# Attention scores of a two-layer graph network: each product of 128 keys made as two of 64 keys

## The chip, the core and the metric

The kernel runs on one core of a Trainium2 chip. Its time is the device time of one execution in microseconds (us), the median of several runs. The core has TensorE (in the profile PE for matrix products and PEld for the loading of their weights), VectorE (DVE), ScalarE (ACT), GpSimd (POOL) and SyncE (SP, which issues DMAs here). Matrix products read SBUF and write PSUM[...].

## What is computed

x has 16 graphs of 1,024 nodes with 256 features; adj is a 1,024 by 1,024 matrix. There are two layers, each added to its input. The change lies in the attention of the first; all of it is in f32.

```python
# --- layer 0 ---
h = jnp.maximum(_layernorm(x, axis=-1), 0.0)
...
Wg = adj[None, :, :] * A_s
g = jnp.einsum('bcn,bnm->bcm', fea, Wg)
g = jax.nn.relu(g * para.reshape(1, C, N))
q = jnp.transpose(g, (0, 2, 1)).reshape(B, N, h, hd).transpose(0, 2, 1, 3)
kv = (x @ kv_w).reshape(B, N, 2, h, hd).transpose(2, 0, 3, 1, 4)
k, v = (kv[0], kv[1])
scale = (1.0 + 1e-06) / (np.sqrt(hd) + 1e-06)
attn = jax.nn.softmax(jnp.einsum('bhnd,bhmd->bhnm', q, k) * scale, axis=-1)
out = jnp.einsum('bhnm,bhmd->bhnd', attn, v)
...
# --- layer 1 ---
h = jnp.maximum(_layernorm(x, axis=-1), 0.0)
...
out = h @ W2.T + b2
out = _batchnorm(out, g2, be2)
```

Layer 1 aggregates over the normalised adj and makes two products, each followed by a batch norm. There are 4 heads (h) of 64 features (hd). So for every graph and head the scores are a product over 64 features, of 1,024 queries with 1,024 keys.

## The kernel before

One pass of `layers` does everything. Its long middle part is `attention`, which for graph b makes scores and values, and lays beside them, piece by piece, the work of other graphs: the queries, keys and values of graph b+1 (`queries`, `keys_values`; tiles pg, pk, pv), and the second layer's aggregation and first product of graph b-1 (`aggregate`, `hidden`; tiles pa, py). A last part, `second`, makes the second product of layer 1 after batch norm (tiles m_f), with the reference's batch statistics.

The order of PE's work is written out by hand. `attention` goes through steps. There are 16 graphs, 2 pairs of heads k and 2 blocks f of 512 queries, 64 units in all; a unit has four steps g, each with two blocks m of 128 keys. In a step PE is given, in this order:

- `scores`: for each of the two blocks m a PSUM tile sc of 128 keys by 2 heads by 512 queries (two banks, one for each head e). The keys of a pair of heads lie in the same SBUF tile, head e in partitions 64e to 64e+63, and the queries likewise. So each head's product contracts over 64 rows and uses one half of the array's rows (L890). ACT then takes the exponential of the whole sc tile into pr (L898). The pool of sc has two buffers, so a tile waits for the exponential of the tile before the last.
- at some steps the small products `sums` (L961) and the transposes `ot` (L986) that end the unit before,
- `values` of the step before: the product of pr with the values into o, 128 keys in the rows and 64 features in the columns, one half of the array's columns for each head (L931),
- one or more pieces of the background, by a planner's costs, until the step's due share is done.

DVE adds the exponentials up for the softmax's denominators (L917, L920).

The background's products go through a helper, `product` (L171), which makes every product of 128 output partitions as two of 64, one in each column half of the array. The helper's two calls differ in the output's partitions and the weights' columns:

```python
        def product(dst, left, right, start, stop):
            for e in range(2):
                r = slice(e * HW, (e + 1) * HW)
                nc.tensor.matmul(dst[r], left[:, r], right, start=start, stop=stop)
```

HW is 64, P is 128, FB is 512 and HD is 64. The products of `second` (L1235) are not split. The program's other branch, `layers(True)` with `shifted_attention`, is taken only where the exponentials leave their range, and isn't in the profile.

Of the kernel before, what the change touches and what calls it, by code (L numbers as in the profile page):

```python
# [17 lines left out]
P = 128  # L18
# [5 lines left out]
def gnn_two_layers_kernel(  # L24
# [12 lines left out]
    nc = tc.nc  # L37
# [6 lines left out]
    FB = 512  # L44
# [3 lines left out]
    HW = P // 2  # L48
# [47 lines left out]
    def layers(shifted):  # L96
# [23 lines left out]
        xs, hs, hts, ats, qs, ks, vs = {}, {}, {}, {}, {}, {}, {}  # L120
# [761 lines left out]
        def scores(b, k, f, g):  # L882


            made = []
            for m in (2 * g, 2 * g + 1):
                sc = ps_sc.tile([P, 2, FB], F32, tag="sc", name=f"sc_{b}_{k}_{f}_{m}")
                for e in range(2):
                    r = slice(e * HD, (e + 1) * HD)
                    nc.tensor.matmul(  # L890
                        sc[:, e, :],
                        ks[b][k][r, m * P : (m + 1) * P],
                        qs[b][k][r, f * FB : (f + 1) * FB],
                        start=True,
                        stop=True,
                    )
                pr = p4.tile([P, 2, FB], F32, tag="p", name=f"p_{b}_{k}_{f}_{m}")
                nc.scalar.activation(pr, sc, AF.Exp)  # L898
                made.append(pr)
            return made  # L900
# [107 lines left out]
        def attention():  # L1008
# [7 lines left out]
            for s in range(len(steps) + 2):  # L1016
                if s < len(steps):
                    unit, g = steps[s]
                    b = unit.at[0]
                    if s % per_graph == 0:  # L1020
                        run(bg)
                        top = False
                        bg, done = background(b), 0.0
                        total = (37.6 if b > 0 else 41.0) * (b + 1 < B) + 24.0 * (b > 0) + 6.0 * (b + 2 < B)
                        total += 13.7 * (0 < b < B - 2) + 27.4 * (b == B - 1) + 3.0 * (b == 0)

                        total -= 10.3 * (b == B - 1)
                    made = scores(*unit.at, g)
                    due = total * (s % per_graph + 1) / per_graph
                else:  # L1030
                    due += 5.1
# [408 lines left out]
```

## Time and profile before

| | |
|---|---|
| time, median of 3 runs | 2608.92 us (2606.27 to 2610.16) |
| span of the profiled execution, first to last instruction | 2604.3 us |
| mean granted TensorE clock | 0.991 |
| sc passes (executed matmuls of L890) | 2048 |
| exponentials p (L898, ACT) | 512, mean 1020 ns |
| passes of the values o (L931) | 2048 |
| DMA rate over the span | 140 GB/s |

An f32 product of the program is executed as two passes, each with a weight load of its own: 1,024 score products are 2,048 matmuls and 2,048 weight loads in the profile. The form 64*128 is the rows and columns of the array that a pass uses; 64x512 after it is the moving operand, partitions by elements. Of a group, "busy" is the union of its instructions' times, and "mean" that of one. Matmuls are pipelined and their ends are modelled, so for the pace of PE the starts are to be read.

### The profile page before, as it was taken

How to read it: one execution, taken by the hardware profiler on the slowest of the kernel's cores; microseconds unless marked ns; L12 is line 12 of the kernel's file. 1: busy time of each engine (PE TensorE's matmuls, PEld its weight loads, DVE VectorE, ACT ScalarE, POOL GpSimd, SP SyncE). 2: the span in 40 equal slices, each digit the busy share in tenths (PEclk: the TensorE clock that was granted, in tenths of full speed). 3: DMA queues.
4: the chain of work that ended last, by engine and by line, in shares of the span. 5: the costliest groups of instructions: out<-in, count | busy, mean ns of one | idle time of the engine just before them, and what ended most of it. 6: DMA issues, size and time to landing. Idle time of an engine off the chain costs nothing.

```text
span 2604.3 us, 31375 instructions
## 1 busy us (share of the span) xinstructions
PE 2525.9 (97%) x11627; PEld 931.8 (36%) x11627; DVE 1822.7 (70%) x2837; ACT 1460.7 (56%) x2034; POOL 391.3 (15%) x456
## 2 busy tenths in 40 slices
PE   7999999999999999999999999999999999999994
PEld 3333333333333333333333333333333333334443
DVE  4768686867767686868677676858686776657774
ACT  6774565647474746656464747465564634335543
POOL 1540001000101000010001010000100001036653
PEclk9999999999999999999999999999999999999997
DMA  3654224152524343241525243433315242355459
GB/s 138 229 171 173 93 99 154 54 189 73 182 83 152 111 148 101 102 150 55 183 71 182 86 156 107 147 100 114 137 62 180 66 166 105 109 196 221 170 198 367
DMA packets 130915, 363.46 MB, mean 140 GB/s; under 512 B 15288, under 2 KB 32192, under 8 KB 124608
## 3 DMA queue, kind: packets, MB, share of 16 engines
q1 hardware_dynamic: 110144, 282.70, 31.3%
q0 software_dynamic: 20608, 78.66, 7.9%
q8 instruction: 94, 1.54, 0.2%
q14 instruction: 69, 0.57, 0.1%
HBM read 286.79 MB, written 74.51 MB: 139 GB/s over the span
## 4 chain that ended last, share of the span: by engine, by line
PE 87%; ACT 7%; DMA 2%; issue 2%; DVE 1%; SPq 0%; POOL 0%; POOLq 0%; DVEq 0%; ACTq 0%
PE sc L890 17%; PE o L931 16%; PE pa L171 15%; PE pg L171 14%; PE py L171 8%; PE m_f L1235 7%; PE pk L171 4%; PE pv L171 4%; ACT w L458 3%; DMA out_dram<-xo_f 2%; ACT p L898 2%; PE ot L986 1%; ACT w L466 1%; PE sums L961 1%; ACT ht L399 1%
## 5 line engine op out<-in xcount | busy, mean ns | idle before, releaser
L898 ACT ACTIVATE p<-sc 128x1024 f32<-128x1024 f32 x512 | 495.0, 1020 | 452.5 <-PE sc L890 452.1
L920 DVE TENSOR_TENSOR acc<-acc,p 128x1024 f32<-128x1024 f32 x384 | 472.2, 1230 | 143.2 <-ACT p L898 121.8
L890 PE MATMUL sc<-q,k 64*128 64x512 f32 x2048 | 509.0, 615 | 4.7 <-ACT p L898 4.6
L931 PE MATMUL o<-p,v 128*64 128x512 f32 x2048 | 495.9, 605 | 0.0
L171 PE MATMUL pg<-w,h_a 128*64 128x512 f32 x1600 | 357.9, 592 | 3.1 <-DVE q L612 2.3
L171 PE MATMUL pa<-aht,h_b 128*64 128x512 f32 x1536 | 344.0, 592 | 3.5 <-ACT h_b L341 3.4
L890 PEld LDWEIGHTS sc<-q,k 64*128 64x128 f32 x2048 | 175.9, 186 | 325.5 <-issue 284.4
L458 ACT ACTIVATE w<-cbc,csum 128x512 f32<-128x512 f32 x256 | 285.5, 1168 | 0.0
L171 PE MATMUL py<-at,w 128*64 128x512 f32 x1024 | 232.8, 597 | 8.4 <-ACT ht L399 7.0
L445 DVE SCALAR_TENSOR_TENSOR w<-w,adj 128x1024 f32<-128x1024 f32 x128 | 157.5, 1230 | 114.8 <-ACT w L466 110.8
L931 PEld LDWEIGHTS o<-p,v 128*64 128x64 f32 x2048 | 124.1, 136 | 250.3 <-issue 247.2
L171 PEld LDWEIGHTS pg<-w,h_a 128*64 128x64 f32 x1600 | 114.7, 137 | 232.0 <-issue 214.4
L746 POOL DMA_DIRECT2D y_d<-y x128 | 70.5, 551 | 795.0 <-ACT y L745 787.2
L171 PEld LDWEIGHTS pa<-aht,h_b 128*64 128x64 f32 x1536 | 110.8, 137 | 216.9 <-issue 208.3
L745 ACT ACTIVATE y<-py,vec 128x512 f32<-128x512 f32 x128 | 87.6, 684 | 142.3 <-PE py L171 119.7
L749 DVE BATCH_NORM_STATS2 stats<-y 128x6 f32<-128x512 f32 x128 | 85.7, 687 | 79.6 <-ACT y L745 79.5
L466 ACT ACTIVATE w<-w 128x1024 f32<-128x1024 f32 x128 | 135.2, 1056 | 1.7
L520 DVE TENSOR_TENSOR w<-w,w 128x1024 f32<-128x1024 f32 x112 | 132.8, 1217 | 1.5
L341 ACT ACTIVATE h_b<-x,lnsm_b 128x256 f32<-128x256 f32 x128 | 70.4, 609 | 110.7 <-DVE lnsm_b L330 110.7
L93 POOL TENSOR_SCALAR lnsm_b<-mv_b 128x4 f32<-128x4 f32 x32 | 12.1, 379 | 791.5 <-DVE mv_b L319 791.4
L171 PEld LDWEIGHTS py<-at,w 128*64 128x64 f32 x1024 | 72.2, 137 | 162.4 <-issue 129.8
L171 PE MATMUL pk<-ht,kvw_f 128*64 128x512 f32 x512 | 117.0, 599 | 1.5 <-ACT ht L399 1.5
(158 smaller groups left out, 2779.7 us busy)
## 6 DMA issues: line engine op xcount, KB each, us to landing
aht<-aht_d SPq DMA_DIRECT2D x224, 512.0 KB, 6.3
adj<-in_adj_dram SPq DMA_DIRECT2D x128, 512.0 KB, 4.4
y_d<-y POOLq DMA_DIRECT2D x128, 256.0 KB, 2.6
yin_f<-y_d SPq DMA_DIRECT2D x32, 1024.0 KB, 6.3
x<-in_x_dram SPq DMA_DIRECT2D x32, 512.0 KB, 5.1
para<-in_para_dram SPq DMA_DIRECT2D x64, 256.0 KB, 3.9
x_d<-x POOLq DMA_DIRECT2D x16, 1024.0 KB, 10.3
xo_f<-x_d SPq DMA_DIRECT2D x32, 512.0 KB, 8.6
```

What stands on the lines that cost most here:

```text
L171: nc.tensor.matmul(dst[r], left[:, r], right, start=start, stop=stop)
L445: nc.vector.scalar_tensor_tensor(w, w, 1.0, a, op0=ALU.add, op1=ALU.mult)
L458: nc.scalar.activation(w[:, t, :].rearrange("p (t q) -> p t q", q=P), cbc[:, q * NT // NH : (q + 1) * NT // NH], AF.Abs, bias=csum[:, th * ...
L466: nc.scalar.activation(made[i], made[i], AF.Tanh, scale=-0.5 / C)
L520: nc.vector.tensor_sub(block(i)[part], block(x)[part], block(y)[part])
L745: nc.scalar.activation(y, made, AF.Identity, bias=b1[:, j : j + 1])
L749: nc.vector.bn_stats(stats1[:, j, i, :], y)
L890: nc.tensor.matmul(sc[:, e, :], ks[b][k][r, m * P : (m + 1) * P], qs[b][k][r, f * FB : (f + 1) * FB], start=True, stop=True,)
L898: nc.scalar.activation(pr, sc, AF.Exp)
L920: nc.vector.tensor_add(self.acc, self.acc, pr)
L931: nc.tensor.matmul(self.o[r, :], vs[b][k][:, m, r], pr[:, e, :], start=(m == 0), stop=(m == NT - 1),)
L1235: nc.tensor.matmul(made, left[:, j, :], right[:, j, :], start=(j == 0), stop=(j == JH - 1))
```

## The change

Each score product is made as two. The inner loop takes the keys of a block in two halves of 64 (c), which are the weights of one pass each, and writes them to partitions 0 to 63 and 64 to 127 of the same bank. With the row halves that the two heads use already, a product takes one quarter of the array, 64 rows by 64 columns. The exponential, the values and all else read and write the same tiles as before, and the order of the other instructions is the same on every engine.

```diff
                 sc = ps_sc.tile([P, 2, FB], F32, tag="sc", name=f"sc_{b}_{k}_{f}_{m}")
                 for e in range(2):
                     r = slice(e * HD, (e + 1) * HD)
-                    nc.tensor.matmul(
-                        sc[:, e, :],
-                        ks[b][k][r, m * P : (m + 1) * P],
-                        qs[b][k][r, f * FB : (f + 1) * FB],
-                        start=True,
-                        stop=True,
-                    )
+                    for c in range(2):
+                        part = slice(c * HW, (c + 1) * HW)
+                        nc.tensor.matmul(
+                            sc[part, e, :],
+                            ks[b][k][r, m * P + c * HW : m * P + (c + 1) * HW],
+                            qs[b][k][r, f * FB : (f + 1) * FB],
+                            start=True,
+                            stop=True,
+                        )
                 pr = p4.tile([P, 2, FB], F32, tag="p", name=f"p_{b}_{k}_{f}_{m}")
                 nc.scalar.activation(pr, sc, AF.Exp)
```

## The prediction

> **What bounds the kernel now.** I read the busy shares first, then the groups, then the order of TensorE's work in one stretch of the attention, since a busy PE says nothing yet of where its time goes.
>
> ```profile
> PE 2525.9 (97%) x11627; PEld 931.8 (36%) x11627; DVE 1822.7 (70%) x2837; ACT 1460.7 (56%) x2034; POOL 391.3 (15%) x456
> ```
>
> PE is at 97% and no other engine is above 70%. The windows of the attention (columns: stretch, its length, then busy us and instructions of PE, PEld, DVE, ACT and POOL, then clock and DMA) say the same without the ends:
>
> ```profile
> 600.00:1000.00 400.00, 398.62 (x1910) 141.63 (x1908) 290.97 (x457) 226.09 (x320) 29.23 (x44) 1.00 0.35 123
> ```
>
> So between some 60 and 2,260 us PE sets the pace, at the full clock. PE is also 87% of the chain that ended last, with ACT 7% and issue 2%. The groups by form show how the products are made (x is executed instructions; an f32 product of the program is executed as two passes, each with its own weight load):
>
> ```profile
> L890 PE MATMUL sc<-q,k 64*128 64x512 f32 x2048 | 509.0, 615 | 4.7 <-ACT p L898 4.6
> L931 PE MATMUL o<-p,v 128*64 128x512 f32 x2048 | 495.9, 605 | 0.0
> L171 PE MATMUL pg<-w,h_a 128*64 128x512 f32 x1600 | 357.9, 592 | 3.1 <-DVE q L612 2.3 <-ACT k L632 0.9
> L171 PE MATMUL pv<-kvw_f,ht 128*64 128x256 f32 x1024 | 116.1, 379 | 0.0
> L1235 PE MATMUL m_f<-yin_f,combined_f 128*128 128x512 f32 x128 | 57.5, 592 | 0.0
> ```
>
> The reader is to see two things. A whole product of 128 rows by 128 columns costs two passes at 57.5/128 = 449 ns (m_f, unsplit) or four at 357.9/1600 = 224 ns (pg, column halves): 898 and 895 ns. Splitting by columns alone buys no array time, because two halves run side by side and each pass lasts as long as before. Second, the scores cost 509.0/2048 = 249 ns a pass where pg costs 224. What the 25 ns are is in the order of PE's work (start, length, group, xcount):
>
> ```profile
> 1003.02 5.32 PE L171 MATMUL py<-at,w 128*64 128x512 f32 x24
> 1008.27 1.99 PE L890 MATMUL sc<-q,k 64*128 64x512 f32 x8
> 1010.18 1.94 PE L931 MATMUL o<-p,v 128*64 128x512 f32 x8
> 1011.95 0.60 PE L171 MATMUL py<-at,w 128*64 128x512 f32 x2
> ```
>
> Read the starts, not the lengths (the ends carry a modelled tail). In the steady state a pair of passes starts every 429 ns: 12 pairs of py should take 5.15 us and take 5.25 until sc starts, so about 0.09 is lost on the way from column halves to row halves. Four pairs of sc should take 1.72 and take 1.91; four of o take 1.77 and pass into py, also in column halves, with nothing lost. What the sc run loses lies at its two ends. The durations of single passes split it up:
>
> ```profile
> L890 PEld LDWEIGHTS sc<-q,k x2048: 182/186/187, 61.6 to 2261.2; 64*128 64x128 f32 x187
> L890 PE MATMUL sc<-q,k x2048: 589/589/693, 61.6 to 2261.6; 64*128 64x512 f32 x187
> L931 PEld LDWEIGHTS o<-p,v x2048: 132/137/137, 67.1 to 2267.5; 128*64 128x64 f32 x187
> L931 PE MATMUL o<-p,v x2048: 592/592/644, 67.1 to 2268.0; 128*64 128x512 f32 x187
> ```
>
> (minimum/median/maximum in ns.) The longest score pass is 693 - 589 = 104 ns over the usual one, the longest o pass 644 - 592 = 52: at the start of a run nothing hides the weight load, and 128 columns cost 104 where 64 cost 52. Taken over the whole trace every run of scores is 8 passes long, so there are 2048/8 = 256 runs, and their 693s are 2 passes a run. From its first pass to the next instruction a run lasts 1.918 us: 4 x 0.429 = 1.716, the load 0.104, and some 0.09 until the array is empty for the next shape. That is 256 x 1.918 = 491 us, 19% of the span, on PE's path.
>
> **What the Trainium skill says.** TensorEngine Tiling (Array Packing), Key Properties: changing the tiling mode, not just the tile, drains TensorE, and tiles work independently. The trace agrees on the drain: about 0.09 us each way. TensorE: Matmul & The Clock Gate, LDWEIGHTS: a load takes its columns divided by 1.2 ns, whatever the rows; for 128 and 64 columns 107 and 53, and the trace has 104 and 52. The same page, Part 3: row and column tiles compose, and sixteen small tiles were measured side by side, while matmuls start strictly in the order of the program. No 64x64 tile stands in this trace, and only two tiles ever run at once, so it can show neither. PSUM Pressure on the tiling page: row tiles must not share a PSUM bank at one time; here e picks the bank and c only the partitions of it, so that is kept.
>
> **The change part by part.** Removed: 1,024 program matmuls of 64 rows by 128 columns. Added: 2,048 of 64 by 64. Order and waits elsewhere stay: the wait for a free sc stands on the first of four instead of the first of two, the signal on the last. Nothing moves on ACT, DVE, POOL or the DMA queues.
>
> 1. Array time. Per score tile there are eight passes instead of four, each still 512 columns of q, 429 ns. If four run side by side that is 2 x 429, as before: 0. The moving operand is then read by four tiles of 64 rows, as many rows as the two tiles of 128 rows in pg, which keep 429.
> 2. Exposed weight load at the start of a run: 104 becomes 52. 256 x 0.052 = -13.3 us.
> 3. Later starts: two neighbouring tiles start 6 to 7 ns apart, so the fourth starts some 20 ns after the first instead of 7. Inside a run each tile keeps its own pace and this vanishes; at the end of a run the next shape waits for the last: 256 x 0.013 = +3.3 us.
> 4. Issue: 16 executed instructions (loads and passes) in 858 ns, 54 ns each. pv already runs 2,048 in 116.1 us, 57 ns each with its tails. Taken at 0; if issue fell short by 5 ns each, 16 x 512 x 0.005 = 41 us would be lost, which is why the range is open upward.
> 5. Drains at both ends of a run: the shapes still differ (64x64 against 128x64 or 128x128). Taken at 0. Bound below: were a change of row halves alone free, 252 entries out of column-split products would save 0.09 + 0.05 and 114 exits into o the same, some -50 us; bound above 0.
> 6. ACT gets sc 13 ns later and 52 ns earlier; DVE follows. Hidden.
>
> Sum -13.3 + 3.3 = -10.0 us. About 9% of the chain is ACT and issue, where a faster PE waits instead (py for ht, sc for p): -9.1. On the profiled execution 2604.3 becomes 2595.2. That execution's span lies 4.6 below the median of 2608.92, which I take for what lies around it: forecast 2599.8.
>
> **Rivals.**
> - *A: the four weight loads don't run side by side.* For: every load in the trace has at most one partner. Against: two row halves load together, and two column halves too. If the row halves of one column half take turns, step 2 is 0 and step 3 stays: +3.3, 2612. If all four take turns, 208 instead of 104: 256 x 0.117 = +30, 2639.
> - *B (slower): the second row half starts a pass late.* Place: the start of each run. The program lists both column halves of row half 0, each two passes, and only then row half 1. If PE interleaves the two passes of neighbours in pairs only and then keeps order, row half 1 starts with the second passes of row half 0. In a run this fills up again, and only its ends stay half empty: one more 429 ns a run. 256 x (0.429 - 0.039) = +100 us, 2709. It decides from a delay of 39 ns. For it: matmuls keep order, and the trace has never interleaved more than two. Against: both tiles of a pair start together on the first pass already, which shows that PE reaches past a second pass that is blocked.
> - *C: the change doesn't do what it says, two passes at a time is all there is.* Every score tile then takes 4 x 429 instead of 2 x 429: 512 x 0.858 = +439, less 13, 3035. For: nothing in the trace has four. Against: two row tiles and two column tiles each work with no loss, and neither the reading (pg) nor the writing (two banks at a time, as now) is more than is shown.
> - *D: the drain gets cheaper too.* Step 5's bound: about 2550. Against: any change of shape costs the same 0.09 in this trace.
>
> **How the numbers follow.** Forecast 46%, A 18%, B 18%, C 14%, D 4%. The likeliest gives 2599.8. Its own range is 2594 (all of step 2, no cost) to 2606 (half of it). The overall range must leave out no more than 2 in 10; with C and D outside it is 2591 to 2714. A measurement of this kernel can tell 0.2%, 5.2 us. Faster by more: 41 of the forecast's 46 and D, 45%. Within: 5 of the forecast and 12 of A, 17%. Slower: 6 of A, B and C, 38%.
>
> **What would show it.** Right: sc passes of 64*64, 16 a run; four starting within some 20 ns; the longest some 52 over the usual; about 1.88 us from the first pass of a run to what follows. A: the longest 104 or more over the usual. B: 2.3 us a run. C: 3.6 us a run and some 900 us of sc. D: py of 24 passes leaving after 5.15 instead of 5.25 us. It would be wrong altogether if passes in steady state were no longer 429 ns apart (issue, or reads that collide).

## The result, and the profile after

| | before | changed |
|---|---|---|
| time, median of 7 runs | 2609.3 us (2606.27 to 2610.16) | 2601.52 us (2599.16 to 2602.98) |
| ratio | | 0.9971, 95% interval 0.996 to 0.9981 |
| span of the profiled execution | 2604.3 us | 2597.8 us |

The changed kernel is faster by 7.8 us, 0.3%. The page after, first the busy shares, then two of its groups (busy us, mean ns of one, idle time before):

```profile
PE 2519.7 (97%) x13675; PEld 887.5 (34%) x13675; DVE 1823.0 (70%) x2837; ACT 1460.5 (56%) x2034; POOL 392.9 (15%) x456
...
L892 PE MATMUL sc<-q,k 64*64 64x512 f32 x4096 | 500.3, 604 | 3.3 <-ACT p L900 3.3
...
L892 PEld LDWEIGHTS sc<-q,k 64*64 64x64 f32 x4096 | 131.4, 132 | 345.4 <-issue 306.4
```

There are twice as many score passes, each about as long as before (mean 604 ns, before 615), and they take slightly less of PE together. So four passes run side by side where two did. The order of PE's work in one stretch (start, length, group, xcount):

```profile
1000.50 5.32 PE L171 MATMUL py<-at,w 128*64 128x512 f32 x24
1005.75 1.95 PE L892 MATMUL sc<-q,k 64*64 64x512 f32 x16
1007.63 1.94 PE L933 MATMUL o<-p,v 128*64 128x512 f32 x8
1009.39 1.89 PE L171 MATMUL py<-at,w 128*64 128x512 f32 x8
```

By the starts, py's 24 passes again take 5.25 us and o's eight 1.76. Only the run of scores is shorter: 1.88 us where it was 1.91. Over all 256 runs the median from the first pass to what follows is 1.878 us, before 1.918. Where the 40 ns lie is seen in the weight loads (PEld). Before (start, length, group, xcount):

```profile
1008.27 0.30 PEld L890 LDWEIGHTS sc<-q,k 64*128 64x128 f32 x4 [0.81 <-issue]
1008.80 0.19 PEld L890 LDWEIGHTS sc<-q,k 64*128 64x128 f32 x2 [0.23 <-issue]
```

and after:

```profile
1005.75 0.21 PEld L892 LDWEIGHTS sc<-q,k 64*64 64x64 f32 x8 [0.81 <-issue]
1006.23 0.15 PEld L892 LDWEIGHTS sc<-q,k 64*64 64x64 f32 x4 [0.28 <-issue]
```

The first row of each holds the loads for the first two passes of every tile; the next load goes in as the second pass begins. That is 0.53 us after the start of the run before and 0.48 after, where 0.43 would be a pass with no load to wait for. By the single instructions, the median starts of a run's passes were 0, 7, 533, 540, 962 ns and so on, and are now 0, 7, 13, 20, then 480, 487, 493, 500, then 909: 53 ns gained, 13 given back by the fourth tile.

Not all of 256 x 0.040 = 10.2 us arrives in the profiled span, which is 6.4 shorter. (The medians differ by more, 7.8. The changed kernel's profiled execution took 2599.8 us, 2.0 more than its span; with the same 2.0, that of the kernel before took 2606.3, near the fastest of its seven.) Cutting PE's time from each start to the next and adding it up by name gives sc 491.1 to 482.5 us, pv 112.3 to 114.3, and all others within 0.4 of before. Two things took something back. First, pv (the values of the next graph) waits for ACT. Of the view of the tile pv, the idle time of PEld that ACT's copy v ended (us, times), before:

```profile
  ACT v L649: 2.8, 13
```

and after:

```profile
  ACT v L649: 5.0, 13
```

pv takes turns in the two PSUM buffers of the background, and its third tile in a graph needs the first copied out by ACT. ACT's work before that copy, in the changed kernel (start, length, group):

```profile
1514.76 1.23 ACT L508 ACTIVATE q<-q 128x512 f32<-128x512 f32 x2 [0.36 <-DVE q L506]
1515.90 1.92 ACT L900 ACTIVATE p<-sc 128x1024 f32<-128x1024 f32 x2
1517.71 0.65 ACT L649 COPY v<-pv 128x256 f32<-128x256 f32 x2
```

The copy comes after two exponentials, and these after two activations of q that waited for DVE. DVE has by then worked for 34.4 us with no pause over 0.3 us, in each of the 13 graphs and in both kernels. By the traces, then, the wait begins at DVE, though its share of the span is 70%, and a faster PE doesn't shorten that stretch. PE has four runs of scores beside it, which save 4 x 0.04 = 0.16 us, and the wait has grown by 2.2/13 = 0.17: what PE saves there is lost whole.

Second, one run of scores fell into a half clock. The windows (stretch, length, busy us of the five engines, granted clock, DMA) of the kernel before:

```profile
167.00:170.50 3.50, 3.17 (x18) 1.68 (x18) 2.81 (x3) 3.50 (x6) 0.00 (x0) 1.00 0.38 137
```

and of the changed one, with the run that it hit below:

```profile
167.00:170.50 3.50, 3.35 (x16) 0.79 (x16) 2.99 (x3) 3.50 (x6) 0.00 (x0) 0.51 0.31 116
```

```profile
167.15 3.59 PE L892 MATMUL sc<-q,k 64*64 64x512 f32 x16 [2.46 <-ACT p L900]
```

From its start to the next instruction at 170.67 us it takes 3.52 us instead of 1.88, a loss of 1.6. So sc should be 10.2 - 1.6 = 8.6 lower, as found.

### The profile page after: what moved, and what is told of

Its sections match the earlier page's. It is cut to its first block, busy times and chain, and to the rows that moved or that the text cites. A ratio compares the mean times of both kernels' runs of the same rounds, so it can differ in the third digit from the quotient of the medians.

```text
span 2597.8 us, 35471 instructions
## 1 busy us (share of the span) xinstructions
PE 2519.7 (97%) x13675; PEld 887.5 (34%) x13675; DVE 1823.0 (70%) x2837; ACT 1460.5 (56%) x2034; POOL 392.9 (15%) x456
## 4 chain that ended last, share of the span: by engine, by line
PE 84%; ACT 7%; DVE 3%; DMA 3%; issue 2%; SPq 0%; POOL 0%; POOLq 0%; ACTq 0%; DVEq 0%
PE sc L892 15%; PE o L933 15%; PE pa L171 15%; PE pg L171 14%; PE m_f L1237 7%; PE py L171 6%; PE pv L171 4%; PE pk L171 4%; ACT w L458 3%; DMA out_dram<-xo_f 2%; ACT p L900 2%; PE ot L988 1%; ACT w L466 1%; DVE acc L922 1%; PE sums L963 1%
## 5 line engine op out<-in xcount | busy, mean ns | idle before, releaser
L892 PE MATMUL sc<-q,k 64*64 64x512 f32 x4096 | 500.3, 604 | 3.3 <-ACT p L900 3.3
L892 PEld LDWEIGHTS sc<-q,k 64*64 64x64 f32 x4096 | 131.4, 132 | 345.4 <-issue 306.4
```

The costliest lines, as they stand in the source:

```text
L892: nc.tensor.matmul(sc[part, e, :], ks[b][k][r, m * P + c * HW : m * P + (c + 1) * HW], qs[b][k][r, f * FB : (f + 1) * FB], start=True, sto ...
```

## The experiments

My theory: the gain is the halved weight load that the start of each run exposes, less the later start of the fourth tile, and the price of every change of the array's shape is left as it was. The rivals are that the order or number of tiles made the gain, that halves are faster in themselves, and that the shape change got cheaper. All diffs are against the changed kernel; each is timed against the kernel before on its own chip, and where two changed kernels are compared, that reference differs by at most 0.5 us.

### Another order of the four quarters

```diff
-                for e in range(2):
-                    r = slice(e * HD, (e + 1) * HD)
-                    for c in range(2):
-                        part = slice(c * HW, (c + 1) * HW)
+                for c in range(2):
+                    part = slice(c * HW, (c + 1) * HW)
+                    for e in range(2):
+                        r = slice(e * HD, (e + 1) * HD)
```

> The four quarters of a score tile in another order: column half 0 of both heads, then column half 1 of both, instead of head by head. My theory (four tiles keep their own pace, only the exposed weight load of a run has changed): first starts again at 0, 7, 13 and 20 ns, a run of scores 1.88 us, the time that of the changed kernel, 2601 us within 3. Rival (it is the neighbours in the program that are interleaved, so the order decides who runs side by side): the second pair starts about one pass later, 2.3 us a run, 2700 us.

Measured: 2601.18 us, ratio 0.9969 (0.9957 to 0.9981). The order of PE's work:

```profile
1007.32 1.95 PE L892 MATMUL sc<-q,k 64*64 64x512 f32 x16
1009.20 1.94 PE L933 MATMUL o<-p,v 128*64 128x512 f32 x8
```

A run is 1.88 us, and its first passes start at 0, 7, 13, 20 and 480 ns, as before the swap. Whichever tiles are neighbours in the program, all four run at once.

### Keys in four quarters

```diff
-                    for c in range(2):
-                        part = slice(c * HW, (c + 1) * HW)
+                    for c in range(4):
+                        part = slice(c * SQ, (c + 1) * SQ)
                         nc.tensor.matmul(
                             sc[part, e, :],
-                            ks[b][k][r, m * P + c * HW : m * P + (c + 1) * HW],
+                            ks[b][k][r, m * P + c * SQ : m * P + (c + 1) * SQ],
```

SQ is 32.

> Keys in four quarters of 32 columns instead of two halves of 64: eight tiles of 64 rows by 32 columns. My theory: the exposed load of a run falls from 52 to about 26 ns, but the eighth tile starts some 47 ns after the first instead of 20, so a run again takes 1.88 us and the time stays at 2601 within 4. Rival 1 (issue is close to its limit): 32 executed loads and passes now fall on 858 ns, 27 ns each; if 54 ns, the most that the trace had shown, is the limit, a run doubles and the time is 3040 us. Rival 2 (the gain came from using more and smaller tiles, not from the load): a further gain of about 8 us, 2593.

Measured: 2602.24 us, ratio 0.9974 (0.9963 to 0.9985). The tile sc (minimum/median/maximum in ns) and a run:

```profile
L892 PEld LDWEIGHTS sc<-q,k x8192: 102/106/107, 63.0 to 2256.8; 64*32 64x32 f32 x200
L892 PE MATMUL sc<-q,k x8192: 589/589/1057, 63.0 to 2257.3; 64*32 64x512 f32 x200
```

```profile
1007.34 1.95 PE L892 MATMUL sc<-q,k 64*32 64x512 f32 x32
1009.21 1.94 PE L933 MATMUL o<-p,v 128*64 128x512 f32 x8
```

The load fell by another 27 ns (133 to 106), and the eighth tile starts 47 ns after the first instead of the fourth 20 ns after it. The two cancel and the run is 1.878 us again. So the gain isn't one of number or smallness of tiles, it is a trade of columns to load against starts in a row, and two halves are as good as four quarters. It also settles issue: 32 loads and passes in 858 ns, 27 ns each, lose nothing.

### Two shapes in one score tile

```diff
-                    for c in range(2):
-                        part = slice(c * HW, (c + 1) * HW)
+                    for c in range(2 - e):
+                        n = HW if e == 0 else P
+                        part = slice(c * n, (c + 1) * n)
```

> Only head 0 is split into two column halves, head 1 stays one product of 64 rows by 128 columns, so that two shapes alternate within a score tile. If any change of shape empties the array and loads anew: head 0 and head 1 no longer run side by side, a run is 8 passes of 0.429 with four drains of 0.09 and four loads (0.052 or 0.104), 4.1 us instead of 1.88, 3170 us. Rival (tiles in separate row halves are free of each other whatever their width): 2605 us.

Measured: 3152.77 us in one run. The order of PE's work:

```profile
1500.85 4.19 PE L893 MATMUL sc<-q,k 64*64 64x512 f32 x12
1504.96 1.51 PE L934 MATMUL o<-p,v 128*64 128x512 f32 x6
```

A run is 4.11 us. The median starts of its passes are 0, 7, 480, 487 (head 0), 1006, 1539 (head 1 alone), 2058 and so on: from 487 to 1006 are a pass of 429 and a drain of 90, and the next 533 are a pass and the 104 of a load of 128 columns. Tiles in separate row halves don't run side by side when their shapes differ. The four quarters are fast because all four have one shape.

### Whole products in the background

```diff
-            for e in range(2):
-                r = slice(e * HW, (e + 1) * HW)
-                nc.tensor.matmul(dst[r], left[:, r], right, start=start, stop=stop)
+            nc.tensor.matmul(dst, left, right, start=start, stop=stop)
```

> The scores as in the changed kernel, but the helper of the background makes whole products of 128 by 128 instead of column halves. My theory (what shape changes and exposed loads cost is all there is): each step now has a change of shape between o and the background, which had none: 252 x (0.09 drain + 0.104 load) = +49 us, 2650. Rival (halves are no better than whole products, a change of columns alone is no change of mode): 2602 to 2606.

Measured: 2644.97 us, ratio 1.0141 (1.0125 to 1.0156), 43 us over the changed kernel where 49 were forecast. The order of PE's work and the passes of pg (minimum/median/maximum in ns):

```profile
1007.40 1.94 PE L931 MATMUL o<-p,v 128*64 128x512 f32 x8
1009.26 5.42 PE L169 MATMUL pa<-aht,h_b 128*128 128x512 f32 x12
1014.61 1.95 PE L890 MATMUL sc<-q,k 64*64 64x512 f32 x16
```

```profile
L169 PE MATMUL pg<-w,h_a x800: 592/592/697, 31.7 to 2127.5; 128*128 128x512 f32 x160
```

o's eight passes now take 1.86 us to the next start instead of 1.76: the drain of 0.09 that a change of shape adds. The first pass of a stretch is up to 105 ns long over the usual: the load of 128 columns, which no pass of another shape hides. In the sum by names o grows by 22 us and the background by 22. A stretch of 12 whole passes takes 5.35 us, of which 0.1 is that load, where 24 halves took 5.25. A change of columns alone is a change of shape too, and no other saving by the halves is seen.

### The sums in the shape of o

```diff
-                nc.tensor.matmul(
+                product(
                     pt,
                     same.rearrange("p a r -> p (a r)"),
                     self.part.rearrange("p e c -> p (e c)"),
-                    start=True,
-                    stop=True,
+                    True,
+                    True,
                 )
```

> The changed kernel, with the product of the sums (128 columns of weights, between a run of scores and the values o) also made in two column halves, the shape of o. My theory (a change of shape costs a drain of 0.09 us and what is exposed of the load): from sums to o there is no change of shape any more and the load falls from 0.10 to 0.05, so the way from the first sums pass to o shrinks from 0.338 us to some 0.17, 49 times; where transposes follow the sums (14 times) there is a new change of shape, 0.1 more. About -9 us, 2592. Rival (such small products in between hide the drain that would be paid anyway, so the way to o stays as long): 2601 us.

Measured: 2594.27 us (2592.05 to 2594.88), ratio 0.9943 (0.993 to 0.9957): the fastest version, 7 us under the changed kernel. The changed kernel's PE around the sums:

```profile
1557.71 1.04 PE L892 MATMUL sc<-q,k 64*64 64x512 f32 x8
1558.68 0.41 PE L963 MATMUL sums<-part,same 128*128 128x32 f32 x2
1559.02 1.94 PE L933 MATMUL o<-p,v 128*64 128x512 f32 x8
```

and this one's:

```profile
1553.30 1.95 PE L892 MATMUL sc<-q,k 64*64 64x512 f32 x16
1555.17 0.31 PE L171 MATMUL sums<-part,same 128*64 128x32 f32 x4
1555.31 1.92 PE L933 MATMUL o<-p,v 128*64 128x512 f32 x8
```

From the sums to o it is 0.14 us instead of 0.34; over the trace the medians are 138 and 338, more than forecast (0.17); that o's own load goes in behind the sums would explain it, but isn't shown by itself. In the sum by names the sums fall from 20.9 to 10.9 us. But pv rises by 3.2, and its wait for ACT's copies grows again:

```profile
  ACT v L649: 10.5, 26
```

This counts both engines, 8.2 us of PEld and 2.3 of PE, in the same 13 places. Each of DVE's stretches is 34.4 us long here too. The shares of the chain that ended last, in the changed kernel and then in this one, show what this means:

```profile
PE 84%; ACT 7%; DVE 3%; DMA 3%; issue 2%; SPq 0%; POOL 0%; POOLq 0%; ACTq 0%; DVEq 0%
```

```profile
PE 60%; DVE 19%; ACT 14%; issue 4%; DMA 3%; SPq 0%; POOL 0%; DVEq 0%; POOLq 0%; ACTq 0%
```

Now PE itself waits, and so the chain runs through DVE: ahead of the pv pass at 1515.13 us it follows DVE from 1478 to 1511, then ACT's activation of q, its exponentials and its copy.

### The second part in column halves

```diff
                 for j in range(JH):
-                    nc.tensor.matmul(
-                        made, left[:, j, :], right[:, j, :], start=(j == 0), stop=(j == JH - 1)
-                    )
+                    for e in range(2):
+                        r = slice(e * HW, (e + 1) * HW)
+                        nc.tensor.matmul(
+                            made[r],
+                            left[:, j, r],
+                            right[:, j, :],
+                            start=(j == 0),
+                            stop=(j == JH - 1),
+                        )
```

> The changed kernel, with the products of the second part (m) also in column halves. They stand in one long sequence of their own shape, so by my theory there is no change of shape and hardly an exposed load to save: the m passes keep 429 ns a pair of halves, the time stays at 2601 within 3 us. Rival (halves are faster in themselves): m takes 202 us of PE's timeline, and a gain of the size that the scores had, 2%, would be 4 us or more, 2597.

Measured: 2601.5 us, ratio 0.9973 (0.9962 to 0.9983), the time of the changed kernel. One group of the changed kernel and the same here (busy us, mean ns):

```profile
L1237 PE MATMUL m_f<-yin_f,combined_f 128*128 128x512 f32 x128 | 57.5, 592 | 0.0
```

```profile
L1239 PE MATMUL m_f<-yin_f,combined_f 128*64 128x512 f32 x256 | 58.0, 592 | 0.0
```

Where no change of shape and no exposed load is to be had, halves bring nothing; m takes 202.5 us of PE's timeline in one and 202.6 in the other.

### DVE copies the first values

```diff
+                copy = nc.vector.tensor_copy if g == 0 else nc.scalar.copy
                 for k in range(CC):
-                    nc.scalar.copy(
-                        vs[b][k][:, 2 * g : 2 * g + 2, :], pv[:, :, k * P : (k + 1) * P]
-                    )
+                    copy(vs[b][k][:, 2 * g : 2 * g + 2, :], pv[:, :, k * P : (k + 1) * P])
```

together with the sums in halves.

> As e5_sums, and the first pair of value tiles of each graph copied out of PSUM by DVE instead of ACT. In the changed kernel the third pv product waits 13 times for ACT's copy of v, 5.0 us where before it was 2.8, since ACT has two exponentials to do first. If that wait is where the part of the gain went that is missing in the sum: the wait falls to 3 us or less and the time by some 2 us against e5_sums. Rival (DVE is later than ACT there, being 70% busy): no gain or a loss of a few us.

Measured: 2649.12 us, ratio 1.0156 (1.0142 to 1.017), 55 us slower than with ACT's copies. The rival was right that DVE is later, and its size was underrated. PE's waits (engine line, releaser: us in total, times, longest):

```profile
PE pv L171 <- DVE v L650: 39.0, 13, 3.0
```

The copies went to the engine whose stretch the wait comes from. In the graph near 1550 us PE could go on at 1554.1, but DVE adds up exponentials until 1556.2 and only then copies; PE waits 3.0 us, and so in all 13 graphs. At the end of 11 of these waits the clock is also halved for 3.4 us. So the wait can't be had back in this way; whether less work for DVE in its stretch, or another order of it, would do so wasn't tried.

## Why the prediction was right

- **What bounds the kernel** held in the main: PE set the pace in the attention, and a saving of 40 ns at 256 places arrived, less 2.0 us at pv and 1.6 at half clock. But once in each of 13 graphs DVE's stretch of 34.4 us sets it.
- **Step 1, array time 0.** Four tiles run side by side, each pass 429 ns. The statement of the Trainium skill, TensorE: Matmul & The Clock Gate, Part 3, that row and column tiles compose, which no run had shown here, holds for f32 passes of 64 by 64 and of 64 by 32.
- **Step 2, the load.** Forecast 52 ns a run, measured 53. The second passes start at 480 instead of 533.
- **Step 3, later starts.** Forecast 13 ns a run, measured 13 (starts at 0, 7, 13, 20). The same part gives about 4 ns for each further tile; here it is 6.7.
- **Step 4, issue, 0.** Right, and far from the limit: 27 ns an instruction lose nothing, so the 41 us set against it was too careful.
- **Step 5, drains unchanged.** py again takes 5.25 us to the scores. Shapes that agree in their columns and differ in their rows drain as all others do; rival D falls.
- **Step 6, "Hidden"**, did not hold: DVE doesn't follow, it is busy without a pause ahead of pv, and the 0.17 us that each of 13 graphs loses there comes from it by way of ACT.
- **The discount for ACT and issue** was mis-sized. The sum took off 0.9 us, for waits of py and sc; the profiled execution gave 2.0 back at pv, which it didn't name, and 1.6 to the half clock. For the time, -9.1 was forecast and -7.8 measured, whose interval (5.0 to 10.4) holds it. The two profiled spans differ by less, 6.4, so that so rough a discount came this near is in part luck. A share of the chain says how much of the path belongs to another engine, not which single wait will grow when PE gets faster. That was to be read from PEld's wait for v, which stood at 13 times 0.2 us already, and from DVE's stretch before it.
- **The 4.6 us around the span** were misread: 2.0 lie around it, and the rest is that the profiled execution was a fast one. The forecast difference doesn't depend on it.
- **Rivals.** A: the loads of all tiles run side by side, as four and as eight. B: no tile starts a pass late, in either order; whether PE reaches past a second pass that is blocked, as the prediction took from the starts, no run shows. C: four run at once, not two.

That the load is the cause is shown directly by the starts, and by its trade against the later starts with four quarters; that halves are worth what they save in drains and exposed loads is shown from both sides by the background (+43 us where shapes come to differ) and the second part (no difference where they don't). That DVE is behind the loss at pv is read from the traces and fits the loss when it got the copies; no run took work off its stretch.

## What to carry to other kernels

Count the places where TensorE changes the shape of its tiles, not the products: in this kernel each costs a drain of 0.09 us and the load of the first weights, 0.8 ns a column. Make small products that lie between larger ones in the shape of a neighbour (the sums gave nearly as much as the change itself), give the first product after a change fewer columns to load (halves paid here, quarters brought nothing more), and don't mix shapes that are meant to run side by side. When the bounding engine is made faster, look for the short waits that it already has on another engine, since these are what grows, and follow each back past the engine that it names. Here ACT's copy was only the last link, and the engine to relieve was, by the traces, DVE, busy for 34.4 us on end though only 70% over the span.

## What the runs showed of the hardware that was not expected

- Weight loads of column halves overlap passes in flight in the same rows. The Trainium skill, TensorE: Matmul & The Clock Gate, Part 3, lists from its own traces that loads overlap only when the row group differs, though its account of the mechanism also lets a load into a background weight buffer go ahead; here o's and pg's pairs of passes keep 429 ns with loads of 64 columns going in throughout, and the whole products of pg with loads of 128 columns do too. A load that had to wait would show as the 0.05 or 0.10 us that it adds at the start of a run. Which buffer a load goes to, no trace shows.
- The half clock of 3.4 us near 168 us stands in the profiled executions of the changed kernel and of all experiments but the one with two shapes, and not in that of the kernel before, though PE's idle time ahead of it is alike (2.43 us before, 2.46 after). With the copies on DVE, waits of 3.0 us ended in a half clock 11 times of 13, so the length of a wait alone doesn't decide it. There is one profile of each kernel, and why it falls where it does stays open.
